# Semaphore increments between the squares of an attention product on TensorE

## The chip, the core and the metric

The kernel runs on one core of a Trainium2 chip. A core has five engines, each with its own queue of instructions: TensorE (PE in the profile, its weight loads PEld), VectorE (DVE), ScalarE (ACT), GpSimd (POOL) and SyncE (SP, which only issues transfers here). They run side by side and wait for each other through semaphores. TensorE multiplies on an array of 128x128 cells that can be split in 16 parts of 32x32; it reads from on-chip SBUF and adds up in eight banks of PSUM. The metric is the device time of one execution in microseconds (us), the median of several runs.

## What is computed

Cross-attention of image tokens to a text context and a second, image-prompt context, for two batches:

```python
text, ip = ctx[:, :77], ctx[:, 77:]                 # 77 + 77 context tokens, 1024 wide
q = split_heads(x @ Wq.T, 20)                       # x: (2, 2048, 640); 20 heads of 32
k, v = split_heads(text @ Wk.T, 20), split_heads(text @ Wv.T, 20)
k_ip, v_ip = split_heads(ip @ Wk_ip.T, 20), split_heads(ip @ Wv_ip.T, 20)
out = merge(attend(q, k, v)) + merge(attend(q, k_ip, v_ip))   # softmax(q k^T / sqrt(32)) v, each on its own
return out @ Wo.T + bo + x
```

All of it is in float32.

## The kernel before

Data lie with the contracted dimension on the 128 partitions. The 640 channels are five chunks of 128, each four heads of 32. A pair q of batch b and chunk c (two batches, five chunks, so ten pairs) is worked on in two steps u of 1024 tokens (`step_of`, line 109). In each step TensorE projects queries (`queries`, line 191), multiplies them with the keys (`scores`, line 219), ScalarE copies the scores out (`take`, line 234), VectorE takes maxima and sums, GpSimd subtracts and normalises, ScalarE exponentiates, and VectorE transposes the probabilities in 32x32 squares (`transpose`, line 313). When both steps of a pair are done, the attention product of the pair, `attend` (line 318), multiplies the values with the transposed probabilities.

`attend` is where the change is. The 154 keys of both contexts, padded to 160, are five groups of 32: the rounds k = 0 to 4. In each round 16 matmuls go out, one for each part of the array: r is the group of 32 rows (and the PSUM bank it writes), g the head, that is the group of 32 columns (and of 32 partitions in the bank). Such a matmul is called a square here: 32x32 weights, 512 moving columns. Squares of the five rounds add up in the same place, so a part of the array has five squares in a product, and the order on TensorE is round by round: (r, g) = (0,0), (0,1), ... (3,3), then the same again. A product has 80 squares, the kernel ten products, 800 squares. Each float32 matmul stands in the profile as two passes with a weight load each.

After a product ScalarE copies the four banks out (`take_attention`, line 342; its copies are lines 348 and 352). The outputs are projected with products of the Strassen kind: batch 0 in `product` (line 476) and `last_chunk` (line 462), batch 1 at the end of the kernel in `finish`, whose matmuls are line 841.

The order of the work is written out by hand: `SCHEDULE` is one long list of words, and the loop at its end calls `emit` (line 628) for each in turn. "R2.0@0" is the scores of group 2 of step 0 into the first four banks, "A.3@0" the attention product of pair 3 into the first four, "CA.3" its copy out, "q", "v", "k" projections. Nothing reorders them: each engine executes its instructions in this order, and waits between engines follow from what reads and writes the same tiles. A wait that does not fit into an instruction stands before it as an instruction of its own (EVENT_SEMAPHORE in the profile); a few stand in the first rounds of products.

## Time and profile before

| | |
|---|---|
| median of 3 runs | 499.93 us (499.33 to 500.44) |
| the profiled execution | 499.79 us, its span 498.0 us |
| TensorE busy | 491.1 us of the span, 4114 matmuls |
| attention products (line 325), ten of them | 55.7 us busy on TensorE |
| VectorE, GpSimd, ScalarE busy | 425.7, 425.7 and 243.0 us |
| TensorE clock granted | full, over the whole span |

In the profile a line such as "L325 PE MATMUL out<-in shape xcount | busy, mean | idle before" groups all instructions of one line of the code, one engine and one operation. The chain that ended last is followed back from the last instruction to whatever released it, and shows which engine set the time in each stretch. The timeline lists instructions in order of time, with neighbours of one kind merged: the first number is the start of the first, the second the length of the merged stretch. PEldq is TensorE's sequencer, which sends instructions to the array. The ends of matmuls are modelled; their starts are recorded.

### The profile page before, as it was taken

To read this page: it belongs to the slowest core of one execution; us is meant where nothing else is said; L and a number is where in the kernel's file an instruction comes from. 1 tells how busy PE (TensorE), PEld (TensorE's weight loads), DVE (VectorE), ACT (ScalarE), POOL (GpSimd) and SP (SyncE) were. 2 spreads that over 40 slices of the span, in tenths; PEclk is the share of its full clock that TensorE was granted. 3 is DMA by queue.
4 is the path that set the end of the run, shared out by engine and by line. 5 is a ranking of instruction groups with operands and counts; after the bars stand their busy time and mean duration, and the time that the engine had idled before them with its cause. 6 is when DMAs were issued, how large, how long until landed. Compare 5 with 4: busy or idle time off the path is not lost.

```text
span 498.0 us, 9768 instructions
## 1 busy us (share of the span) xinstructions
PE 491.1 (99%) x4114; PEld 291.1 (58%) x4114; DVE 425.7 (85%) x388; ACT 243.0 (49%) x423; POOL 425.7 (85%) x189
## 2 busy tenths in 40 slices
PE   9999999999999999999999999999999999999997
PEld 4667658558658555457655655744665575444442
DVE  0078998999989899969996888899699999998985
ACT  1276747667757567566616554647473543100000
POOL 0089799999999999998998999899999999397790
PEclk9999999999999999999999999999999999999999
DMA  8985300354253665794074367554524101510026
GB/s 262 355 238 151 108 15 1 86 110 118 57 161 122 177 214 165 247 333 150 1 253 154 123 200 256 151 165 161 200 64 133 45 2 64 169 64 22 0 105 232
DMA packets 66987, 70.15 MB, mean 141 GB/s; under 512 B 3712, under 2 KB 46720, under 8 KB 66944
## 3 DMA queue, kind: packets, MB, share of 16 engines
q1 hardware_dynamic: 66224, 68.81, 44.4%
q8 instruction: 32, 0.52, 0.4%
q10 hardware_dynamic: 720, 0.72, 0.4%
q14 instruction: 11, 0.09, 0.1%
HBM read 58.21 MB, written 11.30 MB: 140 GB/s over the span
## 4 chain that ended last, share of the span: by engine, by line
PE 66%; POOL 15%; DVE 11%; DMA 3%; ACT 2%; issue 2%; SPq 1%; POOLq 0%
PE bank L194 23%; PE bank L841 11%; POOL pb L265 8%; PE bank L325 8%; PE bank L226 8%; PE bank L133 6%; POOL pb L309 6%; PE bank L483 5%; DVE pb L316 4%; PE bank L464 3%; DVE den L297 3%; DVE mx L251 2%; DMA aT<-in_L_xattn_Wk_ip_dram 2%; DMA wq<-in_L_xattn_Wq_dram 2%; PE bank L493 1%
## 5 line engine op out<-in xcount | busy, mean ns | idle before, releaser
L265 POOL TENSOR_TENSOR pb<-pb,mx 128x1848 f32<-128x1848 f32 (+1 forms) x60 | 175.6, 2944 | 32.1 <-DVE mx L251 31.5
L309 POOL TENSOR_TENSOR pb<-pb,rden 128x1848 f32<-128x1848 f32 (+1 forms) x60 | 175.7, 2945 | 13.2 <-DVE rden L304 12.6
L194 PE MATMUL bank<-x,wq 128*128 128x512 f32 x400 | 178.2, 597 | 0.2
L251 DVE TENSOR_REDUCE mx<-pb 128x24 f32<-128x1848 f32 (+1 forms) x60 | 109.8, 1839 | 30.0 <-ACT pb L238 29.6
L272 ACT ACTIVATE pb<-pb 128x1848 f32<-128x1848 f32 (+1 forms) x60 | 94.3, 1578 | 65.6 <-POOL pb L265 65.5
L194 PEld LDWEIGHTS bank<-x,wq 128*128 128x128 f32 x400 | 74.0, 190 | 88.9 <-issue 81.4
L316 DVE STREAM_TRANSPOSE pb<-pb 128x1920 f32<-128x1920 f32 (+1 forms) x60 | 115.4, 1933 | 7.0 <-POOL pb L309 7.0
L297 DVE TENSOR_REDUCE den<-pb 128x24 f32<-128x1848 f32 (+1 forms) x60 | 110.0, 1840 | 11.6 <-ACT pb L272 11.3
L238 ACT COPY pb<-bank 128x462 f32<-128x462 f32 (+1 forms) x240 | 101.9, 536 | 36.7 <-PE bank L226 36.0
L226 PEld LDWEIGHTS bank<-kT,qT 32*128 32x128 f32 x1280 | 46.5, 184 | 23.8 <-issue 16.4
L226 PE MATMUL bank<-kT,qT 32*128 32x154 f32 x1280 | 57.0, 305 | 0.3 <-ACT kT L550 0.3
L325 PE MATMUL bank<-pb,v 32*32 32x512 f32 x1600 | 55.7, 597 | 0.4 <-DVE pb L316 0.3
L133 PE MATMUL bank<-wo_ct,aT 128*128 128x154 f32 x320 | 45.9, 297 | 0.9 <-ACT aT L352 0.4
L204 ACT ACTIVATE qT<-bank 128x512 f32<-128x512 f32 x40 | 23.6, 596 | 46.5 <-PE bank L194 46.5
L133 PEld LDWEIGHTS bank<-wo_ct,aT 128*128 128x128 f32 x320 | 42.9, 188 | 4.4 <-issue 2.4
L325 PEld LDWEIGHTS bank<-pb,v 32*32 32x32 f32 x1600 | 32.1, 103 | 20.8 <-issue 9.5
L464 PE MATMUL bank<-aT,wo_ct 128*128 128x512 f32 x80 | 36.1, 596 | 0.0
L483 PE MATMUL bank<-aT,wo_ct 128*128 128x256 f32 x128 | 32.6, 387 | 0.1
L483 PEld LDWEIGHTS bank<-aT,wo_ct 128*128 128x128 f32 x128 | 23.5, 190 | 7.3 <-issue 3.6
L789 DVE TENSOR_TENSOR x<-x,bank 128x512 f32<-128x512 f32 x36 | 23.1, 681 | 3.4 <-PE bank L841 3.1
L464 PEld LDWEIGHTS bank<-aT,wo_ct 128*128 128x128 f32 x80 | 15.0, 190 | 16.9 <-issue 16.6
L841 PE MATMUL bank<-pb 128*128 128x512 f32 x48 | 22.1, 594 | 0.0
(71 smaller groups left out, 335.1 us busy)
## 6 DMA issues: line engine op xcount, KB each, us to landing
x<-in_x_dram SPq DMA_DIRECT2D x20, 1280.0 KB, 6.8
out_dram<-acc SPq DMA_DIRECT2D x20, 256.0 KB, 2.4
x<-in_x_dram SPq DMA_DIRECT2D x18, 256.0 KB, 5.4
acc<-in_x_dram SPq DMA_DIRECT2D x16, 256.0 KB, 4.1
out_dram<-x SPq DMA_DIRECT2D x15, 256.0 KB, 2.1
v<-scr SPq DMA_DIRECT2D x40, 80.0 KB, 3.3
wq<-in_L_xattn_Wq_dram SPq DMA_DIRECT2D x9, 320.0 KB, 4.9
aT<-in_L_xattn_Wk_dram SPq DMA_DIRECT2D x5, 512.0 KB, 5.4
```

The costliest lines, as they stand in the source:

```text
L133: nc.tensor.matmul(keys_in(out), loaded[n][:, k, :], cT[:, k, :, t, :], start=(k == 0), stop=(k == NCC - 1))
L194: nc.tensor.matmul(pq, wqs[q % 3][:, k, :], xs[place_of(u, h)][:, k, :], start=(k == 0), stop=(k == NC - 1),)
L226: nc.tensor.matmul(ps[g][:, ts(t, 2 * L)], qTs[(u, h)][g * D : (g + 1) * D, ts(st, P)], kT[g * D : (g + 1) * D, c, b].rearrange("p t l -> ...
L238: nc.scalar.copy(keys_of(u, s)[:, :, g], ps[g][:, : n * 2 * L].rearrange("p (n l) -> p n l", n=n))
L251: nc.vector.tensor_reduce(mx, rows_of(u, s), AX.X, ALU.max, negate=by_rows(u, s))
L265: nc.gpsimd.tensor_tensor(rows_of(u, s), rows_of(u, s), maxs[(u, s)].unsqueeze(3).to_broadcast([P, n, 2, L]), ALU.subtract)
L272: nc.scalar.activation(e, e, AF.Exp)
L297: nc.vector.tensor_reduce(dens[(u, s)], rows_of(u, s), AX.X, ALU.add)
L309: nc.gpsimd.tensor_tensor(rows_of(u, s), rows_of(u, s), rdens[(u, s)].unsqueeze(3).to_broadcast([P, n, 2, L]), ALU.mult)
L316: nc.vector.transpose(p, p)
L325: nc.tensor.matmul(pa[r][g * D : (g + 1) * D, :], v4s[q % 2][rows, g, k, :], zones[rows, :, g, k, :], start=(k == 0), stop=(k == NK - 1),)
L483: nc.tensor.matmul(part, w_of[m][:, kp, op], t_of(m, b, i)[:, kp], start=(op == kp == 0 and m in (1, 2, 5)), stop=(op == 1 and kp == 1 and ...
```

## The change

A semaphore named "pause" is allocated. In `attend`, after the square r = g = 0 of round k, TensorE's queue gets k - 1 increments of it: none in the rounds k = 0 and 1, one in round 2, two in round 3, three in round 4. Nothing waits for the semaphore. Each increment is an instruction by itself (of the EVENT_SEMAPHORE kind, with an update and no wait). That makes six a product, 60 in all; no other instruction of any engine is added, removed or moved, and the other semaphores keep their waits.

```diff
     ctx.enter_context(tc.manual_schedule())
+    pause = nc.alloc_semaphore("pause")
 
     def step_of(u):
 
@@ -329,6 +330,9 @@
                         start=(k == 0),
                         stop=(k == NK - 1),
                     )
+                    if r == g == 0:
+                        for _ in range(k - 1):
+                            nc.tensor.sem_inc(pause, 1)
 
     def rows_of_attention(b, c):
```

## The prediction

> **What bounds the kernel now.** I read the page first: busy shares, then the chain that ended last, then the group of the changed line.

> ```profile
> span 498.0 us, 9768 instructions
> ...
> PE 491.1 (99%) x4114; PEld 291.1 (58%) x4114; DVE 425.7 (85%) x388; ACT 243.0 (49%) x423; POOL 425.7 (85%) x189
> ...
> PE 66%; POOL 15%; DVE 11%; DMA 3%; ACT 2%; issue 2%; SPq 1%; POOLq 0%
> ...
> L325 PE MATMUL bank<-pb,v 32*32 32x512 f32 x1600 | 55.7, 597 | 0.4 <-DVE pb L316 0.3
> ```

> TensorE (PE) has work for 99% of the span and carries 66% of the chain, so time added to or taken from it in a stretch where it leads moves the end. The attention products are 55.7 us of that, ten of them, 5.57 us each. The program has 80 squares in a product (5 rounds of 16), 800 in all; the 1600 matmuls say that each fp32 square runs as two passes, each with its own weight load: four entries a square.

> The chain in order of time (start, duration, what) holds seven of the ten products; the first and the last of them, with what follows the last, and one row for a full matmul:

> ```profile
> 35.45 4.29 PE bank L194 x10
> ...
> 69.27 5.58 PE bank L325 x154
> ...
> 427.96 5.14 PE bank L325 x138
> 433.12 0.66 ACT aT L352 x2
> 433.82 5.42 PE bank L841 x12
> ```

> Ten 512-column matmuls take 4.29 us, so one pass streams for 0.43. Each of the 16 squares of a round has its own 32x32 part of the array, so if the parts ran side by side, ten passes would need 4.3 us. A product takes 5.6: some 1.2 us are lost to the order in which squares start. The change touches that order, so I look inside the first product. I number its squares from 0: square 16 opens the second round, 32 the third, 48 the fourth, 64 the fifth. These are answers of the timeline for weight loads, each a window so small that it holds one load; I name the squares below.

> ```profile
> 70.28 0.10 PEld L325 LDWEIGHTS bank<-pb,v 32*32 32x32 f32 x1
> 70.95 0.10 PEld L325 LDWEIGHTS bank<-pb,v 32*32 32x32 f32 x1
> 71.14 0.10 PEld L325 LDWEIGHTS bank<-pb,v 32*32 32x32 f32 x1
> 71.35 0.10 PEld L325 LDWEIGHTS bank<-pb,v 32*32 32x32 f32 x1
> 71.99 0.10 PEld L325 LDWEIGHTS bank<-pb,v 32*32 32x32 f32 x1
> 72.21 0.10 PEld L325 LDWEIGHTS bank<-pb,v 32*32 32x32 f32 x1
> 72.43 0.10 PEld L325 LDWEIGHTS bank<-pb,v 32*32 32x32 f32 x1
> 73.50 0.10 PEld L325 LDWEIGHTS bank<-pb,v 32*32 32x32 f32 x1
> ```

> In this order: the first load of square 17; the second load of square 32, which goes out as that square starts to multiply; then the first loads of squares 33, 34, 49, 50, 51 and 68. From 32 to 33 and from 33 to 34 there are 0.19 and 0.21 us of nothing: these are the gaps beside which the pauses are put. The same small windows on the matmul row show in their first column the oldest pass still running:

> ```profile
> 69.66 1.02 PE L325 MATMUL bank<-pb,v 32*32 32x512 f32 x17
> 70.73 1.02 PE L325 MATMUL bank<-pb,v 32*32 32x512 f32 x17
> 71.80 1.02 PE L325 MATMUL bank<-pb,v 32*32 32x512 f32 x18
> 72.88 1.02 PE L325 MATMUL bank<-pb,v 32*32 32x512 f32 x18
> 69.75 1.18 PE L325 MATMUL bank<-pb,v 32*32 32x512 f32 x16
> 69.78 1.16 PE L325 MATMUL bank<-pb,v 32*32 32x512 f32 x16
> 69.79 1.19 PE L325 MATMUL bank<-pb,v 32*32 32x512 f32 x16
> ...
> L325 PE MATMUL bank<-pb,v x17: 584/612/612, 143.7 to 144.1; 32*32 32x512 f32 x17
> ```

> The first four are the second passes of squares 0, 17, 34 and 51. Each time, the first load of the square **seventeen later** comes 0.62 us behind: 69.66 to 70.28 (17), 70.73 to 71.35 (34), 71.80 to 72.43 (51), 72.88 to 73.50 (68). So the gap is a wait for an old square to leave, a window of a fixed number of entries: square n is let in when square n-17 is through. A second reading fits these four as well: a square that must wait for its part of the array is held 0.43 us, and 0.19 more pass before its successor is let in, 0.62 together. The next three rows, and the last one for how long a pass is recorded (median 612 ns, 0.61), tell them apart. The running group ends at 70.93 to 70.94 up to 70.36, and at 70.98 just after 70.37; so, 0.61 before, the newest square had begun at 70.33 and the next came at 70.37. That is square 21, 0.62 behind the second pass of square 4 (69.75). Its own part had been free since 69.78 + 0.43 = 70.21, so nothing blocked there, and it waited all the same. I take the window as what rules.

> [...]

> **The change, part by part.** It removes and moves nothing. It adds 1 + 2 + 3 = 6 instructions a product, 60 in all, on TensorE's sequencer, behind squares 32, 48 and 64; no engine waits for their semaphore. Their price is not in the trace of before as increments; the nearest rows are the waits of the same opcode on the same sequencer:

> ```profile
> L325 PEldq EVENT_SEMAPHORE  x26: 51/51/7902, 61.4 to 420.3; - x26
> L325 PEldq EVENT_SEMAPHORE  x5: 51/51/51, 143.5 to 143.9; - x5
> ```

> One whose semaphore has arrived takes 51 ns. The five at 143.5 to 143.9 stand four squares apart, about 0.10 to 0.13 us from one to the next; four squares are sent in 0.07 (squares 17 to 20 start between 70.28 and 70.33), so one instruction costs 0.03 to 0.06. Lower bound 0.05, its own duration; upper bound 0.13, the whole distance. I take 0.06.

> *One increment behind square 32.* Square 33's load goes from 71.14 to 71.20. Square 34 is bound to square 17 (70.73 + 0.62), which the pause does not touch: 71.35 as before. Room: 0.21 less 0.02 to send a square, 0.19. A pause of 0.06, or even 0.13, ends in the gap. It costs nothing here because the window is shut.

> *Two behind square 48.* Square 49 goes from 71.99 to 72.11; square 50 is bound to the late square 33 and comes at 72.27 instead of 72.21; square 51 is bound to square 34 and stays at 72.43. Room for two: 72.43 - 71.99 less 0.04, 0.40.

> *Three behind square 64.* Square 65 starts two passes (0.86) after square 49, at 72.85, and goes to 73.03; square 67 is bound to the late 50 and comes 0.06 later; square 68 is bound to 51 and stays at 73.50. Room for three: 73.50 - 72.85 less 0.05, 0.60.

> The late squares are 33, 49, 50, 65, 66 and 67. Those seventeen behind 65, 66 and 67 would be 82 to 84, and a product ends with 79. So nothing late reaches the squares that end the product: **0 us a product**. If that cover is gone, six pauses of 0.06 are 0.36 us a product, 2.5 over the seven on the chain, 3.6 over ten.

> What is late next: square 67 is the last into the first bank, and ScalarE's copy of that bank starts when it is through. Where TensorE then waits for that copy, 0.06 appear:

> ```profile
> 186.05 2.31 ACT L352 COPY aT<-bank 128x256 f32<-128x256 f32 x8 [0.65 <-PE bank L325]
> 187.86 2.37 PE L133 MATMUL bank<-wo_ct,aT 128*128 128x154 f32 x16 [0.43 <-ACT aT L352]
> ```

> Here, and in the chain at 433.12 to 433.82: two places, 0.12 us. The other copies have no such follower in the chain. Sum: 0 + 0.12 us on the profiled execution's 499.79 (span 498.0, 1.8 around it), which lies 0.14 below the median of three runs, 499.93. Forecast **500.0**. The three runs spread from 499.33 to 500.44, so about 0.2% (1.0 us) is what a measurement can tell from no change.

> **Rivals.** *The gaps come from blocked squares (faster).* The second reading: 0.19 is lost behind every square that finds its part of the array busy (33 in the third round, 49 and 50 in the fourth, 65 to 67 in the fifth). Then a pause that lets the part come free pays: 33 at 71.20 and 34 at 71.22, 0.13 earlier; 49 at 72.11, 51 at 72.14, 0.29 earlier; 65 at 73.03, 68 at 73.08, 0.42 earlier. Seven products on the chain give 2.9 us, 497.0; ten give 4.2, 495.7. For it: the growing number of pauses fits the growing number of gaps exactly. Against it: square 21.

> *An increment holds the line until the squares before it have ended (slower).* Then 33 waits for the second pass of 32 (70.95 + 0.43), its 0.59, 0.06 and 0.03 to restart: 72.06, and 34 comes at 72.07, 0.72 late. By the same sum 51 comes at 73.53 (1.10 late) and 68 at 75.05 (1.55 late): 10.9 us over seven products, 510.8. It decides from 0.19 us a pause on. Against it: the waits of the same opcode in the first round take 51 ns with second passes still to come; but those do not increment.

> *It waits only until the second pass of the square before has begun:* 33 at 71.38 + 0.09 = 71.47, 34 at 71.48, 0.13 late; in later rounds the window swallows the rest. 0.9 us over seven, 500.8. [...]

> **How the numbers follow.** No change, window rules (with the cheap hold): 0.50. Blocked squares: 0.27, since four of my five pairs fit it too. Slower: 0.23, of which pauses that lie on the path, 502.4 to 503.5, hold 0.13 and the full hold 0.10. The range takes the first two and the uncovered pauses, 495.7 to 503.5, and leaves out the full hold. For the likeliest alone: 499.3 to 501.0.

> **What would show it.** Right: square 33's load 0.05 to 0.13 later behind square 32, 34 still 0.62 behind the second pass of 17, products of 5.6 us as before, 26 + 60 semaphore instructions at 51 ns on the line. Wrong: 34 following 33 at once (faster, products near 5.1), or products of 5.9 and more.

## The result, and the profile after

The changed kernel takes **503.28 us** (median of 9 runs, 502.00 to 508.07), the kernel before beside it 499.93 (9 runs, 499.33 to 500.45). The ratio is 1.0076, with a 95% interval of 1.0059 to 1.0093: slower by 0.8%, where the prediction had no change. The profiled execution took 502.82 us. The nine times of the changed kernel spread over 6.1 us, those of the kernel before over 1.1; one execution of each was profiled, so what follows explains that one, and what the longer ones lost besides is not shown.

The page of the kernel after, with the lines that answer to those of before (the squares are now line 326, one further on; the lines below them are four further on):

```profile
span 501.0 us, 9828 instructions
...
PE 493.3 (98%) x4114; PEld 290.2 (58%) x4114; DVE 426.0 (85%) x388; ACT 243.2 (49%) x423; POOL 425.7 (85%) x189
...
q8 instruction: 32, 0.52, 0.4%
...
PE 76%; DVE 9%; POOL 8%; DMA 3%; issue 1%; ACT 1%; SPq 1%; ACTq 0%; POOLq 0%
...
L326 PE MATMUL bank<-pb,v 32*32 32x512 f32 x1600 | 58.1, 597 | 1.3 <-issue 0.9
```

The squares are busy 58.1 us in place of 55.7: 2.4 us more, and 0.9 us more idle in front of them, put down to "issue", that is to nothing that the profile shows. Together 3.3 us, about the whole loss (3.35 between the medians, 3.0 between the two profiled spans, where the changed kernel happened to begin its first product 0.23 us sooner). So the time went into the products, as one would expect of a change made there. But not into all of them. This table has, for each product, the time from its first start to the start of the next matmul behind it, in us, read from the starts in the two traces:

| product | 0 | 1 | 2 | 3 | 4 | 5 | 6 | 7 | 8 | 9 | sum |
|---|---|---|---|---|---|---|---|---|---|---|---|
| before | 5.57 | 5.45 | 5.57 | 5.44 | 5.44 | 5.50 | 5.60 | 5.46 | 5.48 | 5.86 | 55.38 |
| after | 5.56 | 5.45 | **5.96** | 5.45 | 5.44 | **5.93** | **7.28** | **6.25** | 5.48 | 5.86 | 58.65 |

Six products hold the same six increments and are unchanged within 0.01 us. Four lost 0.39, 0.43, 1.68 and 0.80 us. A price of the increments would be paid in all ten.

The worst is product 6. Its stretch of TensorE's timeline, before and then after (start, length of the merged stretch, what, and in brackets the idle time before it):

```profile
303.71 5.67 PE L325 MATMUL bank<-pb,v 32*32 32x512 f32 x160
```

```profile
304.26 5.38 PE L326 MATMUL bank<-pb,v 32*32 32x512 f32 x144
310.52 1.09 PE L326 MATMUL bank<-pb,v 32*32 32x512 f32 x16 [0.88 <-issue]
```

Before, 160 passes run without a gap. After, 144 run, the array empties (304.26 + 5.38 = 309.64), and the last sixteen passes, the eight squares 72 to 79, start together at 310.52. In the other three products the array does not run quite empty, but their last squares are late too: from square 72 on in product 5 and from 70 in product 7, in the same burst, 7 ns apart, and the last square, 79, in product 2. These places are not those of the increments, which stand behind squares 32, 48 and 64.

What they have in common is found by counting TensorE's instructions. A square is four entries of its stream (two loads, two passes). The 4114 passes and 4114 loads of the page and the sequencer's own instructions (89 before, 149 after: semaphores and three drains) make 8317 entries before and 8377 after. The first late entries of the four products stand at places 193, 193, 194 and 194 when counted modulo 256. And q8, the page's queue for "instruction", moved 0.52 MB in 32 packets, 16 KB each. If a packet holds a block of 256 entries, the 32 blocks are 8192 entries, the stream but for its beginning. That q8 carries TensorE's stream is also seen across the kernels below: with block ends at those places the next is due at about entry 8384, and every kernel of 8297 to 8377 entries has 32 of these packets, every one of 8421 to 8585 has 33. The burst of product 6 is behind one of these packets, which two windows of the DMA view show (packets, MB, share; the first is product 6 up to 308.0, the second the 1.1 us behind it):

```profile
DMA packets 545, 1.08 MB, mean 293 GB/s; under 512 B 16, under 2 KB 16, under 8 KB 545
...
q1 hardware_dynamic: 545, 1.08, 91.0%
...
q1 hardware_dynamic: 208, 0.42, 99.7%
q8 instruction: 1, 0.02, 5.6%
```

For 3.7 us no block of instructions comes in while the loads of x hold the DMA engines at 91%. The block starts at 308.07, 3.81 us into the product, and takes 0.99; the late squares start 1.46 us behind its end. In products 5 and 7 they start 1.3 and 1.6 us behind theirs.

Where the prediction had looked, in the first product, all is well. The increments by their line (count, minimum, median and maximum in ns, first and last start), then for the third round and for the fifth:

```profile
L335 PEldq EVENT_SEMAPHORE  x60: 51/51/51, 70.5 to 434.7; - x60
...
L335 PEldq EVENT_SEMAPHORE  x1: 51/51/51, 70.5 to 70.5; - x1
...
L335 PEldq EVENT_SEMAPHORE  x3: 51/51/51, 72.6 to 72.9; - x3
```

The first loads of squares 33 and 34, in the timeline of the loads:

```profile
70.90 0.10 PEld L326 LDWEIGHTS bank<-pb,v 32*32 32x32 f32 x1
71.11 0.10 PEld L326 LDWEIGHTS bank<-pb,v 32*32 32x32 f32 x1
```

The increment runs at 70.47, 0.43 us ahead of square 33, since the sequencer is that far ahead of the array. The second load of square 32 is at 70.71, so the gaps to 33 and 34 are 0.19 and 0.21 us, those of before. The three of the fifth round stand 0.154 us apart (72.58, 72.74, 72.89); there square 65 does come later, by 0.35 us, and the product ends no later.

### The profile page after: what moved, and what is told of

The parts are those of the page before. It is cut to its first block, busy times and chain, and to the rows that moved or that the text cites. A ratio compares the mean times of both kernels' runs of the same rounds, so it can differ in the third digit from the quotient of the medians.

```text
span 501.0 us, 9828 instructions
## 1 busy us (share of the span) xinstructions
PE 493.3 (98%) x4114; PEld 290.2 (58%) x4114; DVE 426.0 (85%) x388; ACT 243.2 (49%) x423; POOL 425.7 (85%) x189
## 4 chain that ended last, share of the span: by engine, by line
PE 76%; DVE 9%; POOL 8%; DMA 3%; issue 1%; ACT 1%; SPq 1%; ACTq 0%; POOLq 0%
PE bank L195 28%; PE bank L845 11%; PE bank L326 9%; PE bank L227 9%; PE bank L134 9%; PE bank L487 5%; POOL pb L310 4%; POOL pb L266 4%; PE bank L468 3%; DVE pb L317 3%; DVE den L298 2%; DMA aT<-in_L_xattn_Wk_ip_dram 2%; DVE mx L252 1%; PE bank L497 1%; DMA x<-in_x_dram 1%
## 5 line engine op out<-in xcount | busy, mean ns | idle before, releaser
L326 PE MATMUL bank<-pb,v 32*32 32x512 f32 x1600 | 58.1, 597 | 1.3 <-issue 0.9
L326 PEld LDWEIGHTS bank<-pb,v 32*32 32x32 f32 x1600 | 30.9, 103 | 25.3 <-issue 15.4
L356 ACT COPY aT<-bank 128x256 f32<-128x256 f32 x40 | 11.6, 406 | 22.3 <-DVE aT L831 15.8
```

Source lines behind the costliest of these rows:

```text
L326: nc.tensor.matmul(pa[r][g * D : (g + 1) * D, :], v4s[q % 2][rows, g, k, :], zones[rows, :, g, k, :], start=(k == 0), stop=(k == NK - 1),)
```

## The experiments

Two theories are named by their mechanism throughout: the *pauses* (increments hold up squares) and the *block ends* (any entries that put the end of a 256-entry block into the wrong place make TensorE wait for the next block). "Tiny matmuls" are 32x32 weights with one moving column, four entries each, put among the matmuls at the kernel's start that compute nothing needed.

### 1. Entries without increments, increments without the block ends

The first adds nine tiny matmuls to the kernel before, 36 entries; the second 43, 172 entries. The third adds 43 to the changed kernel.

```diff
+        for _ in range(9):      # 43 in the second and third
+            nc.tensor.matmul(banks[0][:D, :1], warm[:D, :D], warm[:D, :1], start=True, stop=True)
```

> The kernel before, without any increment, with nine tiny matmuls (32x32 weights, one moving column, into a bank that is overwritten later) behind the seven warm-up matmuls: 36 more entries at the start of TensorE's instruction stream, nothing else. Theory F (the stream is fetched in blocks of 256 instructions, and a product that reaches the end of its block in its last squares waits for the next block): the ends of blocks move from square 78 to 69 in product 3, from 73 to 64 in product 8, and from behind the end into squares 72 to 74 of products 2, 5, 6 and 7; at least three products take 5.8 to 7.3 us in place of 5.4 to 5.6 and the time is 501.5 to 505. Theory P (the increments themselves hold up the squares): no increments, so 499.9, at most 0.5 more for the nine matmuls.

> The kernel before, without any increment, with 43 of the same tiny matmuls at the start (172 entries): the end of a block now falls once into each product, at squares 30 to 63, and never into its last sixteen. It is the control for the next run. Theory F: all ten products 5.4 to 5.9 us as before; the time is that of before plus what the tiny matmuls cost at the start, 499.5 to 502. Theory P: the same.

> The changed kernel, all 60 increments in place, with the same 43 tiny matmuls at the start: the end of a block falls at squares 18 to 51 of each product, never into its last squares. Theory F: no product waits, all ten take 5.4 to 5.9 us, and the time equals that of the kernel before with the same 43 matmuls within 0.5 us. Theory P: 3 to 4 us above that control.

Measured, against 500.51 for the kernel before on the same chip: 505.10 (ratio 1.0090, 1.0076 to 1.0104), 504.73 (1.0081, 1.0068 to 1.0095) and 505.10 (1.0093, 1.0080 to 1.0106). The first two lie above the ranges expected (501.5 to 505 and 499.5 to 502). The totals alone tell little, because the start got longer: the first product starts 2.0, 3.3 and 5.7 us later than before in the three profiled executions. Only 1.05, 2.99 and 4.67 us pass from the first tiny matmul to the matmul behind them. The rest is in the projections that follow: their first 512-column passes stand mostly 0.85 us apart in place of 0.43, until 9.8, 11.7 and 14.1 us. In the second kernel the clock granted to TensorE is 0.55 in the window from 8 to 10 us (0.995 over the whole execution); in the other two the trace's record of the clock begins only at 10.2 and 13.9 us (before: at 4.5), so there the lower clock is inferred from the distance of the passes. The products tell the theories apart.

With nine tiny matmuls and not one increment, four products lose time, the four that lose it in the changed kernel: product 2 takes 6.20 us, 5 takes 6.64, 6 takes 6.93, 7 takes 6.76. Product 6 on TensorE's timeline:

```profile
307.42 5.45 PE L325 MATMUL bank<-pb,v 32*32 32x512 f32 x147
313.34 1.08 PE L325 MATMUL bank<-pb,v 32*32 32x512 f32 x13 [0.47 <-issue]
```

It is the picture of the change: the array empties and the last squares come in a burst. With 43, the row of the products on the page is that of the kernel before to 0.1 us, and with 43 and all sixty increments it is the same again:

```profile
L325 PE MATMUL bank<-pb,v 32*32 32x512 f32 x1600 | 55.6, 597 | 0.4 <-DVE pb L316 0.2
```

```profile
L326 PE MATMUL bank<-pb,v 32*32 32x512 f32 x1600 | 55.6, 597 | 0.4 <-DVE pb L317 0.2
```

The ten products take 55.30 us and 55.31: sixty increments cost 0.01 us in the products. The two spans differ by 2.6 us, and 2.4 of these lie ahead of the first product: the 86 passes of the tiny matmuls take 2.99 us in the one, whose clock record has the full clock from 4.8 to 8.2 us, and 4.67 in the other, whose record begins at 13.9.

### 2. The changed kernel with two squares fewer in each product

All increments stay; the eight entries of two squares of the fourth round are gone, so that a product is two entries shorter than before. The sums that these squares belong to lack a part.

```diff
-                for g in range(G):
+                for g in range(G if (k, r) != (NK - 2, G - 1) else G - 2):
```

> The changed kernel, all 60 increments in place, with the last two squares of the fourth round (r = 3, g = 2 and 3) left out of each product, so a part of the attention is missing: eight entries less against six more, so each product starts at the place in its block that it had before, give or take 20. The end of a block falls into late squares only in product 8 (square 76), as in the kernel before. Theory F: no waits of half a microsecond, 499 to 500.5. Theory P: 503.

Measured: 499.39 (0.9982, 0.9973 to 0.9990). The products take 55.02 us, and none waits:

```profile
L326 PE MATMUL bank<-pb,v 32*32 32x512 f32 x1560 | 55.3, 596 | 0.5 <-DVE pb L317 0.3
```

Against before the products are 0.36 us shorter, with twenty squares fewer in all. With the increments where the change puts them, and nothing added elsewhere, no product waits. The whole time is no measure of that here, since this kernel also has less work than before.

### 3. The increments where no square is

Six increments behind the query projection that follows a product, none between squares.

```diff
-                    if r == g == 0:
-                        for _ in range(k - 1):
-                            nc.tensor.sem_inc(pause, 1)
+        owed[0] += 6            # at the end of attend
 ...
+            for _ in range(owed.pop()):     # in queries, behind its matmuls
+                nc.tensor.sem_inc(pause, 1)
+            owed.append(0)
```

> No increment between squares: the six of each product stand behind the first projection of queries that follows it, where TensorE's queue is full (54 in all, the last product has no such projection behind it). Theory F (blocks of 256 entries): the ends of blocks fall on square 73 of products 3, 5 and 6 and 71 of product 7, as with the change (72, 72, 72, 70); where transfers are busy the product waits, at least products 6 and 7 take 5.9 to 7.3 us, and the time is 501 to 503.5. Product 2, whose block now ends behind it, does not wait. Theory P (increments between squares hold them up): 499.5 to 500.5.

Measured: 504.27 against 499.92 (1.0086, 1.0063 to 1.0108), 0.8 above the range expected; 48 increments stand in the trace, not 54, since product 8 has no such projection behind it either. Products 5, 6 and 7 take 6.62, 7.29 and 6.90 us, product 2 takes 5.56, as before. Product 6:

```profile
304.68 5.46 PE L330 MATMUL bank<-pb,v 32*32 32x512 f32 x147
310.96 1.08 PE L330 MATMUL bank<-pb,v 32*32 32x512 f32 x13 [0.82 <-issue]
```

The loss does not need an increment inside a product. It needs the entries ahead of it. How far the sequencer gets ahead of the array in query projections, the trace of before shows in front of products 0 and 6: it met their first waits 7.8 and 8.0 us ahead of the first square, with the array still on the projections. That TensorE's queue is full there, as the expectations here and in section 6 have it, was not measured.

### 4. The traffic beside a product

Two of the transfers of x, 1280 KB each, are left out in the first kernel and three in the second, with all increments in place; the queries that read them are computed from old data.

```diff
     def load_block(u, h):
+        if (u, h) in ((15, 0), (16, 0)):     # (16, 1), (17, 0), (17, 1) in the second
+            return
```

> The changed kernel without the two transfers of 1.25 MB each that run while product 6 does (the blocks of tokens for step 15, half 0, and step 16, half 0; those two projections then use old tokens, so part of the second batch is wrong). The end of the block stays on square 72 of products 3, 5 and 6. If the fetch of the block is late because it shares the 16 transfer engines with them, it starts 1 to 2.5 us into product 6 in place of 3.8 us, the product takes 5.5 to 5.9 us in place of 7.3, products 5 and 7 stay where they were in the changed kernel, and the time falls by 1 to 2 us, to 501 to 502.5. If traffic has no part in it, product 6 stays near 7.3.

> The run without two loads took away transfers that ran beside product 5, not 6. Here the changed kernel goes without the three transfers of 1.25 MB that the trace shows beside product 6 (the blocks of tokens for step 16, half 1, and step 17, both halves; those projections use old tokens, so part of the second batch is wrong). The end of the block stays on square 72 of products 5 and 6. If traffic makes the fetch late: its start moves from 3.8 us into product 6 to under 2.6, product 6 takes 5.5 to 5.9 us in place of 7.3, product 5 stays at 5.8 or more, and the time falls by 1 to 2 us against the changed kernel, to 501 to 502.5. If traffic has no part in it, product 6 stays near 7.

The first: 501.73 against 499.92 (1.0031, 1.0018 to 1.0044). The time is in the range expected, but I had named the wrong product: the transfers left out ran beside product 5, not 6. On the timeline product 5 has lost its wait, and product 6 has kept it (6.93 us):

```profile
261.58 5.57 PE L328 MATMUL bank<-pb,v 32*32 32x512 f32 x160
...
304.02 5.37 PE L328 MATMUL bank<-pb,v 32*32 32x512 f32 x144
309.93 1.09 PE L328 MATMUL bank<-pb,v 32*32 32x512 f32 x16 [0.54 <-issue]
```

The second, with the three that do run beside product 6: 501.75 against 500.36 (1.0033, 1.0020 to 1.0046). Now product 6 is whole and takes 5.58 us, while product 5 waits again (6.30):

```profile
304.34 5.65 PE L328 MATMUL bank<-pb,v 32*32 32x512 f32 x160
```

Two windows of its DMA view, from 304.4 to 305.6 and from 305.64 to 305.7:

```profile
DMA packets 0, 0.00 MB, mean 0 GB/s; under 512 B 0, under 2 KB 0, under 8 KB 0
...
q8 instruction: 1, 0.02, 132.6%
```

The share of 132.6% says only that the packet, which takes 1.27 us on one of 16 engines, is put down whole to a window of 0.06 us. With nothing else under way the block comes 1.31 us into the product instead of 3.81, and TensorE does not wait for it. The block's end is where it was, in square 72: the same end costs 1.68 us with the traffic and nothing without it.

Product 6 carries this proof, not product 5: a single wait differs from execution to execution. Product 2, which has the same entries and transfers ahead of it in the changed kernel, in these two and in that of section 6, lost 0.39, 0.13, 0.22 and 0.41 us, and product 5 lost 0.43 in the changed kernel and 0.80 in the second one here, though nothing near it was changed. Nor is the traffic all that counts: in product 3 of the changed kernel the DMA engines are 81% busy from its start to the start of the packet, and the packet starts at 1.34 us.

### 5. Three times the increments

3, 6 and 9 in place of 1, 2 and 3, and 22 tiny matmuls at the start, to keep the block ends away from the ends of products 2 to 7.

```diff
-                        for _ in range(k - 1):
+                        for _ in range(3 * (k - 1)):
```

> Three times the increments in each place (3, 6 and 9; 180 in all), and 22 tiny matmuls at the start, so that no block ends in the last twenty squares of products 2 to 7 and 9; only these are read. By the prediction's room (0.19, 0.40 and 0.60 us behind squares 32, 48 and 64) and the 0.154 us that an increment takes, 0.46, 0.92 and 1.39 us stick out and a product takes 0.3 to 0.9 us more, 5.8 to 6.4 in place of 5.4 to 5.6. If the sequencer runs far enough ahead of the array at these points, the products stay at 5.4 to 5.6.

One run, 505.6 against 499.92. Products 2 to 7 take 6.07, 5.83, 5.92, 5.98, 6.05 and 5.82 us, each 0.37 to 0.50 more than before, as expected. Product 9, which the expectation reads too, takes 6.65, 0.79 more: its hole is 0.36, and the wait for the copy behind it is 0.66 in place of 0.34. Product 2 on the timeline, with its hole in the fifth round:

```profile
145.34 4.72 PE L326 MATMUL bank<-pb,v 32*32 32x512 f32 x130
150.33 1.15 PE L326 MATMUL bank<-pb,v 32*32 32x512 f32 x30 [0.27 <-issue]
```

So the room behind squares 32, 48 and 64 is real and ends. Nine increments at 0.154 us each are 1.4 us, more than the 0.60 that the prediction found behind square 64; three are 0.46, less than that. The products lose less than the 0.8 us by which nine stick out of that room; what covers the rest was not followed up. (Products 0, 1 and 8 have block ends here, and are left out.)

### 6. A block end in the middle of a product

44 more increments in the changed kernel, eleven behind each of four query projections, to move block ends from square 72 to about 60. (The expectation says 42; the edit adds 44.)

```diff
+            for _ in range({(12, 1): 11, (14, 0): 11, (13, 1): 11, (13, 0): 11}.get((u, h), 0)):
+                nc.tensor.sem_inc(pause, 1)
```

> The changed kernel with 42 more increments of the same semaphore, ten or eleven behind each of the four projections of queries between products 4 and 5, where TensorE's queue is full. They move the end of the block from square 72 of products 5 and 6 and 70 of product 7 to squares 62, 61 and 59; product 2 keeps its end at square 79. Theory F (blocks): products 5 to 7 take 5.45 to 5.65 us in place of 5.9, 7.3 and 6.3, and the time falls from 503.3 to 499.8 to 501 although there are more increments. Theory P (increments cost): 503.3 or more.

Measured: 504.48 against 500.36 (1.0084, 1.0065 to 1.0103), and this was not as expected. The ends were moved to squares 62, 61 and 59, and the waits went with them: products 5, 6 and 7 take 7.19, 6.22 and 7.12 us. Product 6 on the timeline, 0.6 us longer than before and without a hole, because the wait comes earlier:

```profile
306.10 6.29 PE L328 MATMUL bank<-pb,v 32*32 32x512 f32 x160
```

My rule "an end in the last squares waits" is wrong. What all kernels agree on is another rule. A block of 256 entries is 64 squares. With an end at square 72 the block that ends there began at square 9 of the same product, and with an end at 59 to 62 it began 3 to 13 entries ahead of the product: in both cases **one product holds the whole block, or all but a few entries of it,** and uses it up in under 5 us. Such a product can wait; not each of them does. Where a block begins further ahead of the product, the packet of its successor had started, in these kernels, about 1 us or more before the product began (mostly 4 to 25 us), and no product waited. Where a product holds the whole block, the packet of the next one starts only after the product has, but for some cases in products 8 and 9.

These are the products of that kind in the kernels of this study but the one of section 5, by the start of the packet behind the start of the product, with what the product lost against before. Missing are those cases, with an end at squares 60 to 64 in products 8 and 9: there the packet came 5 to 10 us ahead of the product all the same, and nothing was lost.

| block's end at square | packet starts, us into the product | lost, us | where |
|---|---|---|---|
| 69 to 78 | 0.91 to 1.64 | none | before (products 3, 8), after (3), sections 1 to 4 and 6 (3, 8 and, without its traffic, 6) |
| 72 | 2.08 | none | section 4 (first) (5) |
| 70 | 2.61, 2.73, 3.00 | 0.80, 0.80, 0.97 | after, section 4 (first, second) (7) |
| 72, 72 | 2.63, 2.99 | 0.43, 0.80 | after, section 4 (second) (5) |
| 73, 72, 73, 71 | 3.12, 3.23, 3.41, 3.45 | 1.12, 1.14, 1.31, 1.45 | sections 3, 1, 1, 3 (5, 5, 7, 7) |
| 72, 73, 72, 73 | 3.46, 3.62, 3.81, 3.95 | 1.33, 1.33, 1.68, 1.69 | section 4 (first), section 1, after, section 3 (6) |
| 74, 79, 79, 79, 79 | 2.73, 2.48, 2.58, 2.60, 2.71 | 0.63, 0.39, 0.13, 0.22, 0.41 | section 1, after, section 4 (first, second), this kernel (2) |
| 61, 62, 59 | 1.18, 2.53, 2.69 | 0.62, 1.69, 1.67 | this kernel (6, 5, 7) |

For ends near square 72 a packet up to 2.1 us into the product is in time, and from 2.6 us on every tenth that it is later is roughly a tenth lost (equal starts differ by up to 0.4 us). For an end at 61 even a packet at 1.18 us is too late; the DMA engines were 95% busy up to its start, and why it started so early is not shown. In the products of the table no packet starts earlier than 0.91 us into the product; what lets a packet go, no run shows.

### 7. The changed kernel and the kernel before, both with other block ends

If only the block ends matter, moving them by other means should bring both kernels to the same time. The seven full matmuls at the kernel's start, which compute nothing needed, are replaced by fifty tiny ones, 172 entries more, in the changed kernel and in the kernel before.

```diff
-        for _ in range(7):
-            nc.tensor.matmul(banks[0][:, :P], warm, warm, start=True, stop=True)
+        for _ in range(50):
+            nc.tensor.matmul(banks[0][:D, :1], warm[:D, :D], warm[:D, :1], start=True, stop=True)
```

> The changed kernel, all 60 increments in place, with the seven warm-up matmuls of 128x128 replaced by fifty tiny ones of 32x32 by one column: 172 entries more before the first product, as in the run with 43 tiny matmuls, but without their 3 us at the start. The ends of blocks fall on squares 18 to 51. Theory F (blocks): all ten products as long as before, and the whole time back to that of the kernel before, 499.3 to 501, equal to the next run within 0.5 us. Theory P (increments cost): 503, 3 us over the next run.

> The kernel before with the same fifty tiny warm-up matmuls and no increment, as the control: 499.3 to 501 by both theories, if the start takes as long as with the seven large ones.

Measured on one chip against 499.87: 502.91 with the sixty increments (1.0059, 1.0046 to 1.0072), 503.09 without them (1.0063, 1.0051 to 1.0075). The products take 55.34 us in both. That they are equal is what the block ends foretell and the pauses do not. That both are 3 us slower was missed. The first rows of the two chains show fifty tiny matmuls taking 5.49 us, where the seven full ones of the kernel before took 3.35: this is 2.1 of the 2.9 and 2.8 us by which the first product is late.

```profile
1.05 5.49 PE bank L544 x100
```

```profile
1.05 5.49 PE bank L540 x100
```

```profile
1.05 3.35 PE L540 MATMUL bank<-pb 128*128 128x128 f32 x14 [1.05 <-DVE pb L538]
```

Most of the rest is in the thirty passes of projections behind them, which take 15.3 us in place of 13.8 (a wait of 0.41 us for a transfer falls away in return): the first ones stand 0.85 us apart, as in section 1, and the trace's record of the clock begins only at 10.9 and 10.8 us. So this start too has a lower clock, by the same inference.

No version that beats both kernels came out of this.

## Why the prediction was wrong

**The room behind squares 32, 48 and 64, and 0 us a product: right, wherever no wait for instructions came in.** Six products of the changed kernel are unchanged to 0.01 us, 60 increments cost 0.01 us in the products with other block ends (section 1), and the two kernels of section 7 take the same time. Section 5 shows where the room ends.

**The price of an increment, 0.06 us with bounds 0.05 and 0.13: too low.** They stand 0.154 us apart, above the upper bound. Its own duration is 51 ns, as in the row quoted; the rest of the distance was not to be seen in the waits of before. It did not matter, since three of them, 0.46 us, still fit into 0.60.

**Square 33 at 71.20, 0.06 later: wrong, harmless.** It is not late at all, because the sequencer had met the increment 0.43 us before the array asked for the square. Nor is square 49 behind the two increments: it starts 2.78 us into the product, 2.79 before. Only the three of the fifth round reach the array: 65 is 0.35 us late, where the prediction gave it 0.18.

**The copies of the bank, 0.12 us: about 0.02.** The distance from the start of product 3 to the matmul that waits for its copy was 187.86 - 180.92 = 6.94 us and is 187.99 - 181.03 = 6.96; its idle time rose from 0.43 to 0.45:

```profile
187.99 1.19 PE L134 MATMUL bank<-wo_ct,aT 128*128 128x154 f32 x7 [0.45 <-ACT aT L356]
```

From the start of the last product to the matmuls of the output it was 433.82 - 427.96 and is 436.83 - 430.97, 5.86 both times.

**"It removes and moves nothing": the step that failed.** The change moves every entry behind the first increment to another place in TensorE's stream, by six more with each product. The stream came in blocks of 256 entries here (32 packets of 16 KB, and late entries at places 193 and 194 modulo 256), and in the table of section 6 the waits follow the place of a block's end in a product, together with the time at which the next block's packet starts: after the change 0.39, 0.43, 1.68 and 0.80 us in products 2, 5, 6 and 7. The prediction costed the sixty instructions as time on the sequencer and never as length of the stream. The row that would have shown it was on the page of before, unread: "q8 instruction: 32, 0.52, 0.4%", the same as quoted here of after. With it, counting entries, before has a whole block inside products 3 and 8, both without a wait, and after has one inside products 2, 3, 5, 6 and 7. The count has to start from the place, 193, that the waits of the changed kernel gave, and it does not tell which of these products wait.

**The rivals.** None of them is what happened. Blocked squares (faster) falls: the gaps stayed 0.19 and 0.21 us, and no product got shorter. As no square of the third and fourth rounds was held, the fifth decides: 65 came 0.35 us late, and square 68 stood 4.29 us into the product, 4.30 before, where this rival had it 0.42 earlier. That fits the window, and the prediction's reading of it; what sets its depth, no run shows. The 0.03 us to restart, in the sums of both holds, is in the trace of before, where the load behind a wait starts 0.026 us after the wait's end. The full hold (an increment waits until the squares before it have ended) falls: the increments take 51 ns each. The cheap hold (it waits only until the second pass of the square before has begun) falls, since square 34 stayed 0.21 behind 33. The pauses on the path, 502.4 to 503.5, named a time that the result meets, by a mechanism that sections 1, 3 and 7 exclude: 499.93 plus four waits of 0.39, 0.43, 1.68 and 0.80 us, 3.30, and six products at nothing is 503.23, against 503.28. That this lies inside the prediction's range is luck: the range reached so high for a cause that did not act.

## What to carry to other kernels

An instruction that costs nothing where it stands can still cost where it pushes the others, as in the changed kernel, whose products took 58.65 us in place of 55.38: before costing an added or removed instruction at zero on an engine whose stream is long, count the engine's entries, mark the ends of the blocks (each 256th entry here, by the 32 packets of 16 KB and the late entries' places), and see which blocks are used up within one fast stretch (here 64 squares in under 5 us). Here such a stretch lost 0.13 to 1.69 us where the next block's packet, on the instruction queue's row of the profile, was late: for ends near square 72, from 2.6 us into the product on. Other transfers made it late beside product 6 (3.81 us in place of 1.31); busy DMA engines alone do not tell that it will be (81% busy in product 3, and the packet at 1.34 us). When equal pieces of work change by unequal amounts, the edit's own price is not the cause: compare the pieces one by one before forming a theory.

## What the runs showed that I had not expected

The packet of instructions starts as late as 3.95 us into a product with the transfers of x beside it, and at 1.31 us in the same product without them; yet in product 3 it starts at 0.91 to 1.64 us, with the DMA engines 76% and 81% busy until then in the kernels before and after. A block's instructions were used only 1.3 to 1.6 us after the packet's recorded end in the three products of the changed kernel where that was read off. The place of a block's end is worth more than the instructions themselves: nine tiny matmuls at the kernel's start, which delay the first product by 2.0 us, made the ten products together 4.4 us longer, by four waits 140 to 350 us later (59.76 in place of 55.38 us, section 1). And the start of the kernel differs from execution to execution: in sections 1 and 7 the first full passes stood 0.85 us apart for some time, up to 14.1 us into the span, and in section 5, with 22 tiny matmuls, they stood 0.43 apart from 6.3 us on. The record of the clock begins between 4.1 us (section 5) and 13.9 us (section 1, third), and at 4.5 in the kernel before; what sets that time is not shown. Tiny passes took 35 ns each where the record has the full clock for most of them (2.99 us for 86), and 54 and 55 ns where it had not yet begun (4.67 us for 86, 5.49 for 100).
